# Dealing the last batch's shared expert out between the routed experts of a cross-attention and mixture-of-experts kernel

## The chip, the core and the metric

The kernel runs on one core of a Trainium2 chip. A core has five engines with an instruction stream each: TensorE (matmul, PE in the profile, its weight loads PEld), VectorE (DVE), ScalarE (ACT), GpSimd (POOL) and SyncE (SP), which here only issues transfers. Each engine works through its stream in order, and an instruction that waits holds up everything behind it on its engine. Transfers are issued from SP's queue or from GpSimd's and are carried out by 16 DMA engines that both queues share. The metric is the device time of one launch in microseconds (us), the median over runs; lower is better.

## The reference

All numbers are fp32. A batch of 4 sequences of 512 tokens of width 512 goes through a cross-attention layer and then through a mixture of experts; `out` is the sum of the residual and both.

```python
x = x + attention(layernorm(x), ctx)      # 16 heads of 32; 257 image keys and 1344 text keys, two softmaxes, summed
h = layernorm(x)                          # 2048 tokens
idx, w = router(h)                        # sigmoid scores, 3 of 8 groups, then 4 of 32 experts for each token
slots = the first 80 tokens of each expert, in order of token
for e in range(32):                       # routed experts, 512 -> 256 -> 512
    y = (silu(h[slots[e]] @ Wg[e]) * (h[slots[e]] @ Wu[e])) @ Wd[e]
    out[slots[e]] += y * w[slots[e]]
shared = (silu(h @ sg.T) * (h @ su.T)) @ sd.T     # shared expert, 512 -> 512 -> 512, every token
x = x + out + shared
```

## The kernel before

**Order of work.** The whole order is written out by hand: the program issues instructions in the order of its text, and each engine runs its own in that order. Semaphore waits are derived from which buffers and which regions of DRAM an instruction reads and writes. Two writes to overlapping regions of `out` are put in order by a wait, and a scatter to rows that are only known at run time counts as a write to all of `out`.

**Attention.** For each batch `b` there are four groups `c` of four heads each. A group walks over 13 tiles of keys (`t`, lines 632 to 680). For each tile `exps` (L370) makes scores and their exponentials `pT` in a *wide* buffer (128 x 4 x 512, 1 MB). Two tiles later `consume` multiplies them with the values, and one tile later `added` (L391) adds them up for the softmax's denominator; in the last group of a batch these additions run on VectorE. There are five wide buffers, used in turn (`wide`, L130); keys' weights, the output projection's weights `wo`, the shared expert's input `xT` and its hidden layer `hT` use the same five.

**Residual and routing.** `residual` (L446) projects a tile of 128 tokens, adds x, stores the sum `x1` in DRAM (`x1_d`, L461), normalizes it, and stores it in DRAM by rows (`xw_d`) and transposed (`xnT_d`). For the last batch this happens between the units of the shared expert. `routing` (L717) is a list of small VectorE instructions that end in lists of tokens for each expert; `first` is that of the first three batches, `second` that of the last one. The list's items are dealt out between the units: unit `i` may spend up to `(i - 1) * SHARE` in all, by costs that stand in L979. The ranks (L799) are transposes on TensorE that need a result of VectorE.

**Shared expert.** `shared` (L826) makes a list of units. For each batch there are four `gate` and four `up` units (each a projection of four matmul pairs into a PSUM bank, then Silu on ScalarE or a product on VectorE) and four `down` units (a projection, an addition of x1 fetched from DRAM, and a store to `out`). The downs of a batch stand between the gates and ups of the next. The first `xT` is loaded at L700, behind the last attention group. So there are 44 units before the tokens are known, and the four downs of the last batch (`last_downs`) run behind the issue of the first gathers.

**Routed experts.** For each expert `gather` (L877) fetches 80 rows by an indirect transfer on GpSimd's queue, four experts ahead. `turn` transposes them on TensorE two experts ahead, `gate_up` and `down` (L906) are the matmuls, and the 80 rows `y` are added to `out` in DRAM by an indirect transfer with an addition (L914), on GpSimd's queue. The weights of an expert (three transfers of 512 KB on SP's queue, L709) have four buffers of each kind and are loaded three experts ahead. In expert `e`'s turn the program issues `gate_up(e)`, `gather(e + 4)`, `turn(e + 2)`, `down(e - 1)`, and the weights of `e + 3`.

Of the kernel before, what the change touches and what calls it, by code (L numbers as in the profile page):

```python
# [9 lines left out]
F32 = mybir.dt.float32  # L10
# [3 lines left out]
ALU = mybir.AluOpType  # L14
# [4 lines left out]
P = 128  # L19
# [5 lines left out]
NC = D // P  # L25
# [78 lines left out]
def body(ctx, tc, a, ident, mhalf, logits, x1_d, xw_d, xnT_d, den_d, rec_d, out):  # L104
# [6 lines left out]

    w, mid = pool("w", 1), pool("mid", 1)
    kv, cx = pool("kv", 1, early, side="right"), pool("cx", 1, early, side="right")
    pt, hold, row, st = pool("pt", 5), pool("hold", 4), pool("row", 5), pool("st", 3)
    ring = pool("ring", 1, space=PSUM)
    banks = list(range(8))
    later = Later()
# [9 lines left out]
        n = banks.pop(0)  # L127
        return ring.tile([P, 512], F32, name="po", tag=f"bank{n}"), n

    def wide(name):  # L130
        return pt.tile([P, NC, 512], F32, name=name, tag="wide")

    def rowt(name):
        return row.tile([P, D], F32, name=name, tag="row")
# [311 lines left out]
    def residual(b, qt, aoT, wo):  # L446

        i = b * NQ + qt
        rows = slice(i * P, (i + 1) * P)
        t = {}  # L450

        def fetch():
            t["xr"] = load_x(b, qt)
            nc.gpsimd.tensor_tensor(t["xr"], t["xr"], o_b, ALU.add)

        def project_o():
            ps = psum()
            project(ps, lambda k: aoT[:, k, qt * P:(qt + 1) * P], lambda k: wo()[:, k, :])
            t["x1"] = rowt("x1")
            nc.vector.tensor_tensor(t["x1"], ps, t["xr"], ALU.add)  # L460
            nc.sync.dma_start(x1_d[rows, :], t["x1"])  # L461
            t["moments"] = moments(t["x1"])

        def norm():
            t["xn"] = rowt("xn")
            centred(t["xn"], t["x1"], t["moments"])
            nc.sync.dma_start(xw_d[rows, :D], t["xn"])

        def turn():
            ps = psum()  # L470
            for c in range(NC):
                nc.tensor.transpose(ps[:, c * P:(c + 1) * P], t["xn"][:, c * P:(c + 1) * P], ident)
            t["xnT"] = rowt("xnT").rearrange("p (c t) -> p c t", c=NC)
            nc.scalar.copy(t["xnT"], ps.rearrange("p (c t) -> p c t", c=NC))
            nc.sync.dma_start(xnT_d[:, :, rows], t["xnT"])

        def route():
            ps = psum()
            project(ps[:, :E], lambda k: t["xnT"][:, k, :], lambda k: rw[:, k, :])
            nc.vector.tensor_copy(logits[:, i, :], ps[:, :E])  # L480

        return fetch, project_o, norm, turn, route
# [23 lines left out]
    for b in range(B):  # L506
# [94 lines left out]
        for c in range(NC):  # L601
            more = c + 1 < NC
            if more:
                mx = st.tile([P, NQ, NG4, NM], F32, name="mx", tag="mx", bufs=2)
            if b == B - 1 and c == 0:
                sg = weight("shared_gate", tag="q_w")
            if b == B - 1 and not more:
                su, sd = weight("shared_up", tag="v_w"), weight("shared_down", tag="v_img_w")
            fill, done = [], 0
            pTs, outs, pos, g = [], [], [], {}  # L610

            def taken(pos=pos, outs=outs):
                po, n = pos.pop(0)
                o = held("po_s")
                nc.scalar.copy(o, po)
                banks.append(n)
                outs.append(o)

            def consume(t, v=v, pTs=pTs, pos=pos, taken=taken):

                if t in (0, MIX):
                    pos.append(kept())
                if t == MIX:
                    weighted(
                        v, t, pTs[t], (pos[0][0], slice(0, HALF), False, True), (pos[1][0], slice(HALF, P), True, False)
                    )
                else:
                    weighted(v, t, pTs[t], (pos[0][0], slice(0, key_rows(t)), t == 0, t == NKT - 1))
                if t in (MIX, NKT - 1):
                    taken()  # L630

            for t in range(NKT):
                pT = wide("pT")
                pTs.append(pT)
                if more:
                    wave(c + 1, t, qT, kT, mx)
                if t == 0 and c:
                    mT = shifts(part, nc.scalar.copy)
                if t in (0, 2) and pending:
                    pending.pop(0)()  # L640
                if t == 1:
                    if more:
                        v_next = kv.tile([P, NKT, P], F32, name="v", bufs=2)
                        fill = values(v_next, c + 1, cTs, ws)
                        fill[0]()
                        done = 1
                    elif b + 1 < B:
                        fill = work
                if t > 1:
                    consume(t - 2)  # L650
                exps(c, t, qT, kT, mT, pT)
                if t == 0 and pending:
                    pending.pop(0)()
                if t == 2:
                    g["acc"] = begun(pTs, not more)
                elif 2 < t <= MIX:
                    added(g["acc"], pTs[t - 1], slice(0, P), not more)
                elif t == NKT - 1 and not more:
                    added(g["acc"], pTs[MIX], slice(0, HALF), True)
                if c == 0 and t < 3:  # L660
                    rest[t]()
                if c == NC - 2 and b + 1 < B and t and t % 3 == 0:
                    turn[t // 3 - 1][2]()
                while t and done * (NKT - 1) < len(fill) * t:
                    fill[done]()
                    done += 1
                later.step()
                if more and t == NKT - 1:
                    part = parts[(c + 1) % 2]
                    split(mx, part, NM)  # L670
                if c == NC - 2 and b + 1 < B:
                    if t == 0:
                        xs = []
                        qT_next, sq_next, turn, work = queries(b + 1, xs, P)
                    if t % 3 == 0 and t < 3 * NQ:
                        xs.append(load_x(b + 1, t // 3))
                    if t % 3 == 1 and t < 3 * NQ:
                        turn[t // 3][0]()
                    if t % 3 == 2:
                        turn[t // 3][1]()  # L680

            def image(consume=consume, pTs=pTs, idle=not more):

                consume(NKT - 2)
                added(pTs[NKT - 2], pTs[NKT - 1], slice(0, key_rows(NKT - 1)), idle)
                if idle:
                    added(pTs[NKT - 2], pTs[MIX], slice(HALF, P), idle)

            def end(i=b * NC + c, c=c, aoT=aoT, outs=outs, acc=g["acc"], pTs=pTs, idle=not more):
                slabs = [(acc, 0), (pTs[NKT - 2], 2)] + ([] if idle else [(pTs[MIX], 1)])  # L690
                normalize(i, c, aoT, *outs, summed(slabs))

            pending += [image, partial(consume, NKT - 1), end]
            if more:
                v = v_next
            else:
                pending.pop(0)()
        if b + 1 < B:
            qT, sq_q = qT_next, sq_next
    first_xT = wide("xT")  # L700
    nc.sync.dma_start(first_xT, xnT_d[:, :, :L])
    aoT_last = aoT


# [6 lines left out]
        return ws  # L711

    NR = NT - NQ
    SHARE = 2.3
    AHEAD = 4

    def routing(lo, n):  # L717
# [108 lines left out]
    def shared():  # L826

        units = []
        downs = []
        xTs = {0: first_xT}  # L830

        def fetch_x(n):
            xTs[n] = wide("xT")
# [2 lines left out]
        for n in range(B):  # L836
# [11 lines left out]
            def up(ic, n=n, t=t):  # L848
                ps = psum()
                project(ps, lambda k: su[:, k, ic * P:(ic + 1) * P], lambda k: xTs[n][:, k, :])  # L850
                nc.vector.tensor_tensor(t["hT"][:, ic, :], t["hT"][:, ic, :], ps, ALU.mult)

            def fetch(j, n=n, t=t):
                t[j] = held("x1r")
                nc.sync.dma_start(t[j], x1_d[n * L + j * P:n * L + (j + 1) * P, :])

            def down(j, n=n, t=t, fetch=fetch):
                if j == 0:
                    fetch(0)
                if j + 1 < NQ:  # L860
# [3 lines left out]
                nc.vector.tensor_tensor(t[j], t[j], ps, ALU.add)  # L864
                nc.sync.dma_start(out[n * L + j * P:n * L + (j + 1) * P, :], t[j])

            for ic in range(NC):
                units += [partial(gate, ic), partial(up, ic)]
                if n and ic < 2:
                    units += downs[2 * ic:2 * ic + 2]  # L870
            downs = [partial(down, j) for j in range(NQ)]
        return units, downs

    def expert_parts():
        weights, xps, xpTs, hs = {}, {}, {}, {}
# [47 lines left out]

        return weights, gather, turn, gate_up, down

    units, last_downs = shared()
    wo = weight("o_w", wide("wo"))
    for u in units[:2]:
        u()
# [55 lines left out]
    tokens()  # L985
    for e in range(AHEAD):
        gather(e)
    for f in last_downs:
        f()
    turn(0)  # L990
    turn(1)
    for e in range(E + 1):
# [6 lines left out]
        if e:  # L999
            down(e - 1)  # L1000
            if e + 3 < E:
                weights[e + 3] = expert_weights(e + 3)

# [1 line left out]

# [34 lines left out]
```

## Time and profile before

| what | us |
|---|---|
| median of 3 runs | 1780.51 |
| lowest and highest run | 1779.47, 1783.83 |
| the profiled execution, end to end | 1803.62 |
| span of its records | 1801.9 |
| TensorE busy | 1709.7 (95%) |
| VectorE busy | 1002.6 (56%) |
| GpSimd busy | 830.4 (46%) |
| start of the first shared unit's matmuls | 1383.74 |
| start of the tokens' transpose | 1563.80 |
| start of the first expert's transpose | 1577.76 |
| last matmul's end | 1785.98 |

The profile shows one execution, and times in it count from the start of its span. A row of the timeline holds a start, a duration, the engine, the line of the code, what the instruction writes and reads, how many were merged, and in brackets how long the engine had been idle before it and what ended that. A row of waits holds who waited for whom, the total, how often, and the longest. Indirect transfers are issued from GpSimd; their rows show the time of issuing, not that of the transfer.

### The profile page before, as it was taken

What the parts mean: (1) busy time and instruction counts of PE and PEld (TensorE: products, weight loads), DVE (VectorE), ACT (ScalarE), POOL (GpSimd) and SP (SyncE); (2) the same over time, 40 slices, a digit from 0 to 9 for tenths busy, and PEclk for the clock granted to TensorE, in tenths of its full rate; (3) what the DMA queues carried; (4) which work ended last, traced back from release to release, by engine and by line L of the source; (5) the groups of instructions that cost most, each with busy time, mean ns of one, the idle gap of its engine ahead of it and who ended that gap; (6) DMA issues with size and microseconds to landing.
All of it is one profiled execution on the core that took longest, in us unless ns stands there. A gap on an engine that the chain in (4) does not pass through costs nothing. (4 is left out here: it accounts for less than half of the span.)

```text
span 1801.9 us, 29352 instructions
## 1 busy us (share of the span) xinstructions
PE 1709.7 (95%) x11825; PEld 899.0 (50%) x11825; DVE 1002.6 (56%) x1893; ACT 621.7 (35%) x1336; POOL 830.4 (46%) x564
## 2 busy tenths in 40 slices
PE   4999999999999999999999999998999999999886
PEld 2564444445644444565444445643442454477664
DVE  2485666658556657675566558556556668511110
ACT  1114444631254555114554631254456110011111
POOL 1319759322379662327679422377681100123332
PEclk9999999999999999999999999999999999999998
DMA  6000000040100003120001040300011363389894
GB/s 220 1 1 1 20 1 31 15 156 30 65 1 20 31 2 119 50 77 18 20 1 32 14 156 13 105 1 14 2 59 60 114 207 105 100 263 283 272 287 103
DMA packets 68023, 138.38 MB, mean 77 GB/s; under 512 B 16048, under 2 KB 28464, under 8 KB 65584
## 3 DMA queue, kind: packets, MB, share of 16 engines
q1 hardware_dynamic: 62768, 125.70, 20.7%
q0 software_dynamic: 5120, 10.82, 2.9%
q8 instruction: 93, 1.52, 0.3%
q14 instruction: 42, 0.34, 0.1%
HBM read 113.68 MB, written 22.81 MB: 76 GB/s over the span
## 5 line engine op out<-in xcount | busy, mean ns | idle before, releaser
L380 ACT ACTIVATE pT<-ps 128x512 f32<-128x512 f32 (+1 forms) x832 | 429.7, 603 | 385.7 <-PE ps L379 377.4
L342 DVE TENSOR_REDUCE mx<-ps 128x1 f32<-128x512 f32 (+1 forms) x576 | 330.5, 615 | 255.8 <-PE ps L328 255.8
L395 POOL TENSOR_TENSOR acc<-acc,pT 128x1024 f32<-128x1024 f32 x192 | 449.5, 2377 | 14.4 <-ACT pT L380 13.8
L298 PEld LDWEIGHTS ps<-v_w,cT 128*128 128x128 f32 (+1 forms) x1408 | 170.5, 188 | 103.2 <-DVE mx L342 55.3
L387 PE MATMUL po<-pT,v 128*32 128x512 f32 (+2 forms) x1792 | 221.9, 603 | 0.0
L379 PE MATMUL ps<-qT,kT 32*128 32x512 f32 (+1 forms) x1664 | 218.0, 594 | 0.0
L328 PE MATMUL ps<-kT,qT 32*128 32x512 f32 (+1 forms) x1536 | 205.1, 550 | 0.0
L298 PE MATMUL ps<-v_w,cT 128*128 128x128 f32 (+1 forms) x1408 | 199.0, 286 | 0.0
L238 PE MATMUL ps<-cT,wk 128*128 128x512 f32 (+1 forms) x384 | 153.9, 546 | 0.0
L316 DVE TENSOR_REDUCE mx<-ps 128x1 f32<-128x512 f32 (+2 forms) x256 | 128.2, 564 | 7.3 <-PE ps L313 7.2
L914 POOL DMA_INDIRECT out<-y,tok x32 | 45.4, 1420 | 146.4 <-DMA out<-y,tok 72.3
L376 PE MATMUL ps<-mT,pick 32*128 32x512 bf16 (+1 forms) x832 | 86.7, 386 | 23.0 <-DVE mx L342 19.6
L395 POOL TENSOR_TENSOR pT<-pT 65x1024 f32<-65x1024 f32 x24 | 56.0, 2352 | 109.1 <-PE po L387 89.4
L245 POOL TENSOR_TENSOR sq_k<-sq_k,sq 128x512 f32<-128x512 f32 (+2 forms) x48 | 49.6, 1033 | 122.6 <-ACT sq L242 122.6
L376 PEld LDWEIGHTS <-pick 32*128 32x128 bf16 (+1 forms) x832 | 21.8, 91 | 167.4 <-issue 164.1
L238 PEld LDWEIGHTS ps<-cT,wk 128*128 128x128 f32 x384 | 69.6, 190 | 70.5 <-issue 54.3
L904 DVE TENSOR_TENSOR ehT<-ehT,ps 128x160 f32<-128x160 f32 x32 | 10.3, 321 | 164.1 <-ACT ehT L903 164.1
L306 ACT COPY v<-ps 128x128 f32<-128x128 f32 (+1 forms) x208 | 59.7, 287 | 117.4 <-PE ps L298 116.8
L328 PEld LDWEIGHTS ps<-kT,qT 32*128 32x128 f32 x1536 | 80.4, 184 | 31.1 <-issue 10.4
L379 PEld LDWEIGHTS ps<-qT,kT 32*128 32x128 f32 (+1 forms) x1664 | 81.5, 181 | 27.4 <-issue 23.1
L387 PEld LDWEIGHTS po<-pT,v 128*32 128x32 f32 (+2 forms) x1792 | 34.6, 107 | 119.1 <-issue 109.8
L402 POOL TENSOR_TENSOR acc<-pT 128x1024 f32<-128x1024 f32 x24 | 56.7, 2386 | 79.8 <-ACT pT L380 55.3
(176 smaller groups left out, 2187.6 us busy)
## 6 DMA issues: line engine op xcount, KB each, us to landing
W_gate<-in_W_gate SPq DMA_DIRECT2D x32, 512.0 KB, 5.7
W_up<-in_W_up SPq DMA_DIRECT2D x32, 512.0 KB, 6.7
W_down<-in_W_down SPq DMA_DIRECT2D x32, 512.0 KB, 5.5
xt<-in_x SPq DMA_DIRECT2D x32, 256.0 KB, 2.8
cT<-in_ctxT SPq DMA_DIRECT2D x8, 1024.0 KB, 8.4
rb<-rec_d SPq DMA_DIRECT2D x64, 128.0 KB, 2.7
wk<-in_k_w SPq DMA_DIRECT2D x4, 1024.0 KB
wki<-in_k_img_w SPq DMA_DIRECT2D x4, 1024.0 KB, 10.2
```

Source lines behind the costliest of these rows:

```text
L238: nc.tensor.matmul(ps[:, :n], lhsT=wt[:, k, c * P:(c + 1) * P], rhs=xT[:, k, to], start=k == 0, stop=k == NC - 1)
L298: nc.tensor.matmul(ps[lo:hi, :], lhsT=cTs[bl][:, k, at:at + hi - lo], rhs=ws[bl == NB - 1][:, k, c * P:(c + 1) * P], start=k == 0, stop=k ...
L306: nc.scalar.copy(v[:n, t, :], ps[:n])
L316: nc.vector.tensor_reduce(mx[:, qt, g, bl:bl + 1], ps[:, :n], AX.X, ALU.max, negate=True)
L328: nc.tensor.matmul(ps[:, j * n:(j + 1) * n], lhsT=qT[r:r + HD, c, q * P:(q + 1) * P], rhs=kT[r:r + HD, c, k0:k0 + n], start=True, stop=True,)
L342: nc.vector.tensor_reduce(mx[:, qt, g, i:i + 1], ps[:, :m], AX.X, ALU.max, negate=True)
L376: nc.tensor.matmul(ps[:n], lhsT=pick[r:r + HD, kind(t), :n], rhs=mT[r:r + HD, :], start=True, stop=False)
L379: nc.tensor.matmul(ps[:n], lhsT=kT[r:r + HD, c, t * P:t * P + n], rhs=qT[r:r + HD, c, :], start=False, stop=True)
L380: nc.scalar.activation(pT[:n, g, :], ps[:n], AF.Exp)
L387: nc.tensor.matmul(po[r:r + HD, :], lhsT=v[rows, t, r:r + HD], rhs=pT[rows, g, :], start=start, stop=stop)
L395: (nc.vector if idle else nc.gpsimd).tensor_tensor(to[rows, h, :], to[rows, h, :], pT[rows, h, :], ALU.add)
L402: (nc.vector if idle else nc.gpsimd).tensor_tensor(acc[:, h, :], pTs[0][:, h, :], pTs[1][:, h, :], ALU.add)
```

## The change

The last batch's gate, up and down units are no longer part of the shared stage. They are returned as a list `between`, and one of its twelve items is issued at the end of each odd expert's turn, from expert 1 to expert 23. The last batch's `x1` is stored in `out` instead of `x1_d`; its down units copy their result to SBUF on ScalarE, and an accumulating transfer on GpSimd's queue adds it to `out` (128 rows of 2 KB), in place of the fetch of x1, the addition on VectorE and the plain store. The first `xT` is loaded in tile 6 of the last attention group, into one of the five wide buffers, which stays out of the turn until the last unit of the first batch that reads it. With 36 units in place of 44, `SHARE` is 2.9 in place of 2.3.

```diff
--- before.py
+++ after.py
@@ -111,7 +111,7 @@
 
     w, mid = pool("w", 1), pool("mid", 1)
     kv, cx = pool("kv", 1, early, side="right"), pool("cx", 1, early, side="right")
-    pt, hold, row, st = pool("pt", 5), pool("hold", 4), pool("row", 5), pool("st", 3)
+    pt, hold, row, st = pool("pt", 1), pool("hold", 4), pool("row", 5), pool("st", 3)
     ring = pool("ring", 1, space=PSUM)
     banks = list(range(8))
     later = Later()
@@ -127,8 +127,16 @@
         n = banks.pop(0)
         return ring.tile([P, 512], F32, name="po", tag=f"bank{n}"), n
 
-    def wide(name):
-        return pt.tile([P, NC, 512], F32, name=name, tag="wide")
+    wides = list(range(5))
+
+    def wide(name, keep=False):
+
+        n = wides.pop(0)
+        t = pt.tile([P, NC, 512], F32, name=name, tag=f"wide{n}")
+        if keep:
+            return t, n
+        wides.append(n)
+        return t
 
     def rowt(name):
         return row.tile([P, D], F32, name=name, tag="row")
@@ -458,7 +466,8 @@
             project(ps, lambda k: aoT[:, k, qt * P:(qt + 1) * P], lambda k: wo()[:, k, :])
             t["x1"] = rowt("x1")
             nc.vector.tensor_tensor(t["x1"], ps, t["xr"], ALU.add)
-            nc.sync.dma_start(x1_d[rows, :], t["x1"])
+
+            nc.sync.dma_start((out if b == B - 1 else x1_d)[rows, :], t["x1"])
             t["moments"] = moments(t["x1"])
 
         def norm():
@@ -664,6 +673,9 @@
                 while t and done * (NKT - 1) < len(fill) * t:
                     fill[done]()
                     done += 1
+                if b == B - 1 and not more and t == NKT // 2:
+                    first_xT = wide("xT", True)
+                    nc.sync.dma_start(first_xT[0], xnT_d[:, :, :L])
                 later.step()
                 if more and t == NKT - 1:
                     part = parts[(c + 1) % 2]
@@ -697,8 +709,6 @@
                 pending.pop(0)()
         if b + 1 < B:
             qT, sq_q = qT_next, sq_next
-    first_xT = wide("xT")
-    nc.sync.dma_start(first_xT, xnT_d[:, :, :L])
     aoT_last = aoT
 
 
@@ -711,7 +721,7 @@
         return ws
 
     NR = NT - NQ
-    SHARE = 2.3
+    SHARE = 2.9
     AHEAD = 4
 
     def routing(lo, n):
@@ -827,7 +837,7 @@
 
         units = []
         downs = []
-        xTs = {0: first_xT}
+        xTs = {0: first_xT[0]}
 
         def fetch_x(n):
             xTs[n] = wide("xT")
@@ -849,12 +859,21 @@
                 ps = psum()
                 project(ps, lambda k: su[:, k, ic * P:(ic + 1) * P], lambda k: xTs[n][:, k, :])
                 nc.vector.tensor_tensor(t["hT"][:, ic, :], t["hT"][:, ic, :], ps, ALU.mult)
+                if n == 0 and ic == NC - 1:
+                    wides.append(first_xT[1])
 
             def fetch(j, n=n, t=t):
                 t[j] = held("x1r")
                 nc.sync.dma_start(t[j], x1_d[n * L + j * P:n * L + (j + 1) * P, :])
 
             def down(j, n=n, t=t, fetch=fetch):
+                if n == B - 1:
+                    ps = psum()
+                    project(ps, lambda k: t["hT"][:, k, j * P:(j + 1) * P], lambda k: sd[:, k, :])
+                    y = held("ys")
+                    nc.scalar.copy(y, ps)
+                    nc.gpsimd.dma_start(out[n * L + j * P:n * L + (j + 1) * P, :], y, accum_op=ALU.add)
+                    return
                 if j == 0:
                     fetch(0)
                 if j + 1 < NQ:
@@ -864,12 +883,15 @@
                 nc.vector.tensor_tensor(t[j], t[j], ps, ALU.add)
                 nc.sync.dma_start(out[n * L + j * P:n * L + (j + 1) * P, :], t[j])
 
+            if n == B - 1:
+                return units + downs, [partial(f, ic) for ic in range(NC) for f in (gate, up)] + [
+                    partial(down, j) for j in range(NQ)
+                ]
             for ic in range(NC):
                 units += [partial(gate, ic), partial(up, ic)]
                 if n and ic < 2:
                     units += downs[2 * ic:2 * ic + 2]
             downs = [partial(down, j) for j in range(NQ)]
-        return units, downs
 
     def expert_parts():
         weights, xps, xpTs, hs = {}, {}, {}, {}
@@ -923,7 +945,7 @@
 
         return weights, gather, turn, gate_up, down
 
-    units, last_downs = shared()
+    units, between = shared()
     wo = weight("o_w", wide("wo"))
     for u in units[:2]:
         u()
@@ -985,8 +1007,6 @@
     tokens()
     for e in range(AHEAD):
         gather(e)
-    for f in last_downs:
-        f()
     turn(0)
     turn(1)
     for e in range(E + 1):
@@ -1000,6 +1020,8 @@
             down(e - 1)
             if e + 3 < E:
                 weights[e + 3] = expert_weights(e + 3)
+            if e % 2 and between:
+                between.pop(0)()
 
 # ---- launch: one core; the host lays the arrays out ----
```

## Prediction

> **What bounds the kernel now.** The share of busy time (TensorE 95%) is a mean over stages, so I first read the windows of each engine over the last 450 us, the part which the change touches, then the timeline of each of its joints, then who waited for whom. Columns of the windows: busy us and instructions of TensorE, weight loads, VectorE, ScalarE, GpSimd, then granted clock, DMA share, GB/s.
>
> ```profile
> 1400.00:1450.00 50.00, 50.00 (x130) 22.98 (x129) 35.55 (x63) 4.71 (x8) 10.18 (x12) 1.00 0.46 152
> 1450.00:1500.00 50.00, 50.00 (x151) 24.73 (x150) 35.21 (x45) 6.43 (x9) 1.80 (x3) 1.00 0.56 189
> 1500.00:1550.00 50.00, 49.46 (x119) 21.82 (x118) 43.09 (x95) 2.39 (x4) 0.00 (x0) 1.00 0.22 70
> ...
> 1630.00:1680.00 50.00, 44.64 (x290) 34.66 (x289) 5.32 (x14) 7.60 (x15) 16.55 (x15) 0.91 0.89 272
> 1680.00:1730.00 50.00, 45.23 (x306) 35.15 (x305) 5.23 (x14) 6.92 (x14) 16.39 (x14) 0.93 0.90 280
> 1730.00:1786.00 56.00, 50.15 (x326) 37.37 (x324) 6.15 (x16) 8.89 (x18) 19.26 (x16) 0.97 0.72 213
> ```
>
> In the shared-expert stage (to 1564) TensorE never rests and VectorE, which does the routing, is at 71 to 86%. In the expert stage (1578 on) TensorE loses time: clock below 1, DMA at 0.9. The waits of that stage say to whom:
>
> ```profile
> POOL out L914 <- DMA out<-y,tok: 72.3, 18, 6.0
> ...
> PE ps L890 <- DMA xp<-xw_d,tok: 17.7, 11, 2.6
> ```
>
> Each scatter-add (L914) waits on GpSimd for its predecessor to land, the gathers (L879) queue behind it, and TensorE's transpose (L890) waits 17.7 us for gathers. So this stage has two bounds close together. TensorE's own work is 5.53 us an expert:
>
> ```profile
> 1588.59 1.91 PE L232 MATMUL ps<-xpT,W_gate 128*128 128x80 f32 x16
> ...
> 1594.12 1.91 PE L232 MATMUL ps<-xpT,W_gate 128*128 128x80 f32 x16
> ```
>
> 1594.12 - 1588.59 = 5.53, times 32 = 177.0. The stage runs from 1577.8 to TensorE's end at 1786.0, 208.2, so 31.2 is **loss**: waits, and slow matmuls after them. The other bound is the chain of scatters, landing by landing: while weights stream, 4.8 to 8.7 us from start to start where the predecessor's landing was the releaser, mean 6.7; in the tail, without weights, 4.65:
>
> ```profile
> 1709.06 1.42 POOL L914 DMA_INDIRECT out<-y,tok  x1 [5.00 <-DMA out<-y,tok]
> 1710.79 0.93 POOL L879 DMA_INDIRECT xp<-xw_d,tok  x1 [0.30 <-issue]
> 1716.13 1.42 POOL L914 DMA_INDIRECT out<-y,tok  x1 [4.41 <-DMA out<-y,tok]
> ...
> 1789.73 1.39 POOL L914 DMA_INDIRECT out<-y,tok  x1 [3.25 <-DMA out<-y,tok]
> 1794.39 1.39 POOL L914 DMA_INDIRECT out<-y,tok  x1 [3.27 <-issue]
> ```
>
> **Profiled against plain.** That execution took 1803.6 (span 1801.9), 23.1 above the median of 1780.5. Matmuls back to back at 0.43 us can't hide that, so it sits where DMA landings set the pace: the start (0 to 25 us, DMA 0.93) and the expert stage. I put 17 of the 23 in the expert stage (26 scatters x 0.6 = 16, a chain of 6.1 in place of 6.7) and so take the loss in a plain run as 31.2 - 17 = 14. No row splits it; it is my largest unknown.
>
> **Step 1, the early load of the first xT.** Now TensorE meets this:
>
> ```profile
> 1383.74 6.49 PE L232 MATMUL ps<-xT,shared_gate 128*128 128x512 f32 x8 [3.81 <-DMA xT<-xnT_d]
> ...
> 1400.18 3.60 PE L232 MATMUL ps<-xT,shared_up 128*128 128x512 f32 x8
> ```
>
> The wait of 3.81 goes, and eight matmuls take 3.60 in place of 6.49: -6.7. The load takes one of five wide buffers for tiles 7 to 12, so an exp must wait for the additions four tiles back, not five. Tile 6's end at about 1372.7 (two of ten additions of 1.14 from 1370.37) and tile 10's exps start at about 1374.3 (ScalarE's row from 1370.01, 2.16 a tile): hidden with 1.6 to spare; without that cover one addition, 2.3. On SP the load stands behind rec and rb (1362 to 1364) and ahead of wo, which keeps its buffer and time; nothing queues behind it. Range -7 to 0.
>
> **Step 2, twelve units leave the shared stage.** Eight gate and up units before the tokens and four downs behind the gathers (1563.92, 14.00 us): 12 x 3.43 (1403.61 - 1400.18) = -41.2. Four x1 fetches and four stores leave SP, which isn't late there, and the last batch's x1 goes to `out` with the same store as before to x1_d: 0.
>
> **Step 3, routing in fewer units.** The share 2.9 in place of 2.3 deals the same list over units 2 to 31 rather than 39. By the code's own costs (63.9 for the first list, 23.0 for the second) the first ends at unit 23 and the second fills 23 to 31. The second list's VectorE rows add up to about 30 us (maxima and replacements 15, the 128-wide ones 9, small ones 4, gaps 2), evictions of those units add 5 x 0.65: 33.3 against 8 x 3.43 = 27.5 of TensorE. VectorE falls 6 behind; `ranks` (L802) and the first down, which needs the last product, make TensorE wait for it, with 1.5 of slow clock after it. Now it waits 0.54 there: +7. Ends: 0 if evictions catch up in the last four units, +11 if both waits are paid in full.
>
> **Step 4, the gathers lose their cover.** Now 14 us of downs lie between the gathers' issue (1564.5) and the first transpose (1577.8). Afterwards the transpose waits for the gather to land: 3.0 to 5.4 (least and median), I take 4.3. Whether slow matmuls follow, the Trainium skill and the rows see differently. The skill ("TensorE: Matmul & The Clock Gate", Part 1) has half clock only after an idle window of about 3.4 us, so a wait of 3.0 would cost 3.0 and no more. Here the down behind waits of 1.7 to 2.6 us took 2.7 to 3.6 in place of 1.88, six times of seven, 1.3 to 1.7 with the matmuls after it. By the row I add 1.7: +6; by the page's rule and the least landing it is +3. Ends +3 and +9.
>
> To the first transpose: -6.7 - 41.2 + 7 + 6 = **-34.9**.
>
> **Step 5, the units come back between the experts.** One after each odd expert to 23: +41.2 on TensorE. Its products and copies are 0.7 us on engines below 20%: 0. Whether 41.2 can sink into the old loss is the whole question. In the first half, a pair of experts takes 2 x 5.53 + 3.43 = 14.5 on TensorE against 13.4 on the chain: the loss vanishes there. In the second half (experts 16 to 31) four accumulating stores to `out` join the same chain at 17, 19, 21, 23: each waits on GpSimd for the scatter before it, the next gather and scatter wait behind it. The skill ("DMA: Bandwidth & Descriptors", Rules for kernel authors) gives the reason: an accumulate reads and writes later, so it must wait for the earlier DMA on those bytes; the 72.3 us above are that wait, and the row of a full-size store that adds is missing here. Its price: by the same page's fit (Anatomy of one DMA, 2.0 us + bytes / 436 per ns) 256 KB take 2.6. By the nearest row, scatters of 80 rows, least landing 3.8 and median 5.9, it is more for 128 rows. Uncontended, of 4.65 some 3 don't grow, 1.65 x 128 / 80 gives 5.6; contended, 3.6 x 1.6 = 5.8 and 3.0 give 8.8. I take 8.4; ends 3.4 (the page with 0.85 between landing and next issue) and 12.
>
> The second half in a plain run: chain 12 x 6.1 + 4 x 4.65 + 4 x 8.4 = 125; TensorE 16 x 5.53 + 4 x 3.43 = 102. GpSimd may end 7 later than without lag, as it does now (12.2 from TensorE's end to the last landing at 1794.39 + 3.8; 5.5 would do for one store), so the tail stays and 125 - 102 - 7 = 16 come back as loss; slow matmuls are inside it, since the chain sets the pace there. 16 against 14: +2. With the page's 3.4 the chain is 105, the loss 0 and this term -14.
>
> **Sum.** -34.9 + 41.2 + 2 = +8.3: 1780.5 + 8.3 = **1789**. In the profiled execution (chain 6.7, so 133 and a loss of 24 against 31) it would be about -1, so the two profiles may stand closer than the plain times.
>
> **Rivals.** (A) *The chain is the bound in plain runs too*, with a loss of 31, and the moved matmuls fill it. With stores of 6.5 rather than 8.4 the loss afterwards is 24 - 7.6 = 16: -34.9 + 41.2 + 16 - 31 = -9: 1771. For it: 72.3 us of waits, DMA at 0.9. Against: the 23 us. It decides from a plain period of 6.7 with stores below some 7.3. Faster, 0.20. (B) *It all cancels*: a plain period of 6.3 (loss 20) and stores of 7 leave 75.6 + 18.6 + 28 - 109 = 13: -1, 1780; 0.18. (C) *The stores bind harder*: 12 each with gathers behind them, 4 x 3.6 = 14 more: 1803; 0.14. For it: scatters of 8.7 already occur; against, they are few. (D) *The early load does nothing*, because buffer or transfer is late: 1789 + 6.7 = 1796; 0.06; against it stand the 1.6 us worked out above. The forecast has 0.42; with C and D, slower is 0.62. About 0.3% (5.3 us) is what a measurement of this kernel can tell from no change.
>
> The range runs from below A's middle to above C's, leaving out a third of A and half of C: 1768 to 1804. The forecast's own is 1786 to 1796.
>
> **What would show it.** Step 1: no wait on xT, first gate in 3.6. Step 2: twelve projections fewer before the first transpose. Step 3: TensorE waits at L802's transposes and the first down of the third batch, 4 to 11 us. Step 4: a wait for xp of 3 to 5 before the first transpose, which stands near 1543. Step 5: pairs of 14.5 without waits to expert 16, then waits for xp of 2 to 6 us around the accumulating stores; these 7 to 10 us apart from their neighbours; TensorE's end 235 to 250 after the first transpose (208 now). Wrong if the waits for xp in the second half are gone (A), or if VectorE isn't waited for.

## The result, and the profile after

| comparison with the kernel before, on the same chip | before, median (lowest to highest) | after, median (lowest to highest) | ratio, 95% interval |
|---|---|---|---|
| first, 12 runs each | 1782.41 (1779.05–1786.41) | 1807.05 (1788.14–1816.14) | 1.012 [1.0094, 1.0146] |
| second, another chip | 1787.32 (1781.63–1810.29) | 1804.85 (1786.73–1827.65) | 0.9991 [0.992, 1.0062] |

The ratios leave disturbed runs out, which in the second row takes away half of after's six, so its ratio is not that of the two medians beside it. In the first comparison the kernel became slower, by more than forecast: 24.6 us between the medians where the forecast had 8.3, and the median of 1807 stands 3 us above the top of the range (by the ratio, 1.012 x 1780.5 = 1802, it lies just inside). The two rows disagree by more than their intervals allow, and the lowest runs lie only 9 (first) and 5 (second) apart. So besides the change something else moves the time by 20 us and more. The profiles show both parts.

The profiled execution of after took 1808.05 (span 1806.3). First its TensorE timeline from the end of attention to the first experts:

```profile
1384.12 3.70 PE L240 MATMUL ps<-xT,shared_gate 128*128 128x512 f32 x8
...
1508.54 1.01 PE L812 MATMUL ps<-ident,chosen 128*32 128x128 f32 x4 [4.54 <-DVE chosen L790]
...
1544.00 0.80 PE L912 MATMUL ps<-ident,xp 80*128 80x80 f32 x4 [3.90 <-DMA xp<-xw_d,tok]
1545.11 0.77 PE L912 MATMUL ps<-ident,xp 80*128 80x80 f32 x4 [0.31 <-DMA xp<-xw_d,tok]
1545.67 3.62 PE L240 MATMUL ps<-xpT,W_gate 128*128 128x80 f32 x16
1549.08 3.62 PE L240 MATMUL ps<-xpT,W_up 128*128 128x80 f32 x16
...
1556.44 3.62 PE L240 MATMUL ps<-xpT,W_up 128*128 128x80 f32 x16
...
1560.39 3.22 PE L931 MATMUL ps<-W_down,ehT 128*80 128x512 f32 x4
1563.44 3.60 PE L240 MATMUL ps<-xT,shared_gate 128*128 128x512 f32 x8
1566.87 1.91 PE L240 MATMUL ps<-xpT,W_gate 128*128 128x80 f32 x16
...
1581.36 1.91 PE L240 MATMUL ps<-xpT,W_gate 128*128 128x80 f32 x16
```

The wait on `xT` is gone (step 1). TensorE waits 4.54 for VectorE at the ranks (step 3) and 3.90 for the first gather (step 4), and the first transpose starts at 1544.00. But then the gate and up groups of experts 0 and 1 take 3.62 each in place of the 1.91 that they take from 1566.87 on. Only behind the first matmuls that are 512 wide, expert 0's down at 1560.39, are they full speed again. From there a pair of experts with one shared unit takes 1581.36 - 1566.87 = 14.49, as forecast.

The windows of after confirm the clock (columns as in the prediction; the granted clock stands before the last two):

```profile
1545.60:1563.40 17.80, 17.80 (x79) 15.81 (x78) 1.94 (x5) 0.61 (x2) 1.82 (x2) 0.51 0.30 91
1563.40:1680.00 116.60, 116.60 (x707) 83.72 (x706) 14.39 (x36) 18.55 (x37) 37.70 (x32) 1.00 0.81 261
1680.00:1730.00 50.00, 47.65 (x268) 33.38 (x267) 4.42 (x12) 7.96 (x16) 13.01 (x11) 0.93 0.79 240
1730.00:1790.00 60.00, 51.62 (x321) 38.16 (x319) 5.25 (x14) 8.47 (x17) 19.93 (x17) 0.91 0.68 186
```

0.51 for 17.8 us, with TensorE busy all that time; then 116.6 us without any idle time; then losses from 1680 on, where the accumulating stores stand. Who waits there, from the list of waits of after, and TensorE's and GpSimd's rows around two of the four stores:

```profile
POOL out L936 <- DMA out<-y,tok: 36.4, 8, 5.4
POOL out L936 <- DMA out<-ys: 20.1, 4, 6.7
POOL out L875 <- DMA out<-y,tok: 18.2, 3, 6.5
```

```profile
1737.44 0.77 PE L912 MATMUL ps<-ident,xp 80*128 80x80 f32 x4 [2.18 <-DMA xp<-xw_d,tok]
...
1755.87 0.77 PE L912 MATMUL ps<-ident,xp 80*128 80x80 f32 x4 [5.64 <-DMA xp<-xw_d,tok]
...
1786.54 3.60 PE L931 MATMUL ps<-W_down,ehT 128*80 128x512 f32 x8
```

```profile
1742.40 1.44 POOL L936 DMA_INDIRECT out<-y,tok  x1 [1.96 <-ACT y L935]
...
1750.38 0.96 POOL L875 DMA_DIRECT2D out<-ys  x1 [6.54 <-DMA out<-y,tok]
1751.64 0.99 POOL L901 DMA_INDIRECT xp<-xw_d,tok  x1 [0.30 <-issue]
...
1756.14 1.47 POOL L936 DMA_INDIRECT out<-y,tok  x1 [3.52 <-DMA out<-ys]
```

The store at 1750.38 (L875) waits 6.54 for the scatter before it. Behind it stands the gather of expert 28, which is issued 6.5 late and lands at 1755.73, and TensorE's transpose for that expert, at 1755.87, has waited 5.64. TensorE ends at 1786.54 + 3.60 = 1790.1, 246.1 after the first transpose (208.2 before).

**Two parts of the time.** I split each profile at the end of the attention part (where the first shared gate could start). From there to the end of the span, before takes 422.0 and after 422.2; in two further profiles of the unchanged kernels, before takes 415.9 and after 424.5. So the part that the change edits is longer by some 4 us in the mean (419 and 423.4), by 0.2 in one pair and 8.6 in the other. The larger scatter comes from ahead of that point, from 1380 us of which only the buffers' turn in the last group was edited. In the four profiles the attention part ends at 1379.9 and 1382.7 (before) and at 1384.1 and 1401.4 (after). What it follows is one VectorE instruction, the sum at the end of a group (L438 before, L446 after). Timeline of before, GpSimd, VectorE, TensorE:

```profile
218.13 9.27 POOL L395 TENSOR_TENSOR acc<-acc,pT 128x1024 f32<-128x1024 f32 x4
218.51 9.44 DVE L438 SCALAR_TENSOR_TENSOR aoT<-po_s,v_b 128x512 f32<-128x512 f32 x1
228.60 0.58 PE L376 MATMUL ps<-mT,pick 32*128 32x512 bf16 x1 [6.48 <-DVE mx L342]
228.60 2.28 PE L379 MATMUL ps<-qT,kT 32*128 32x512 f32 x8
232.00 2.36 POOL L395 TENSOR_TENSOR acc<-acc,pT 128x1024 f32<-128x1024 f32 x1 [4.59 <-ACT pT L380]
```

And in the kernel of the first experiment below, which has the same code here:

```profile
219.64 16.68 POOL L403 TENSOR_TENSOR acc<-acc,pT 128x1024 f32<-128x1024 f32 x7
220.13 2.40 DVE L446 SCALAR_TENSOR_TENSOR aoT<-po_s,v_b 128x512 f32<-128x512 f32 x1
```

The same instruction on the same shapes takes 9.44 or 2.40. In the long case it ends 0.55 us behind GpSimd's fourth addition (218.13 + 9.27 = 227.40), when GpSimd has no further one to make: the next starts at 232.00. The maxima behind it on VectorE are late, and TensorE waits 6.48 and goes on slowly (eight matmuls in 2.28). The long case comes up at most once in each batch, at its first group:

| profile | long sums, of 4 | end of the attention part |
|---|---|---|
| early_only, cover_two, stores_aside, units_left_out | 0 | 1365.1, 1366.3, 1367.2, 1363.3 |
| before, before_again, after | 2 | 1379.9, 1382.7, 1384.1 |
| stores_together, together_covered | 3 | 1393.2, 1392.4 |
| after_again | 4 | 1401.4 |

(1401.4 - 1365.5) / 4 = 9.0 us each, and the count orders all ten profiles. The names are those of the experiments. That the long sums are the cause rests on this order and on a wait of 6.4 to 6.5 that TensorE has behind each of them, in every profile, and nowhere else; the last experiment takes the instruction away, but brings waits of its own.

### The profile page after: what moved, and what is told of

Its sections match the earlier page's. It is cut to its first block, busy times and chain, and to the rows that moved or that the text cites. A ratio compares the mean times of both kernels' runs of the same rounds, so it can differ in the third digit from the quotient of the medians.

```text
span 1806.3 us, 29363 instructions
## 1 busy us (share of the span) xinstructions
PE 1716.0 (95%) x11825; PEld 906.4 (50%) x11825; DVE 1001.5 (55%) x1889; ACT 623.7 (35%) x1340; POOL 835.4 (46%) x568
## 5 line engine op out<-in xcount | busy, mean ns | idle before, releaser
L387 PE MATMUL ps<-qT,kT 32*128 32x512 f32 (+1 forms) x1664 | 218.2, 594 | 0.0
L926 DVE TENSOR_TENSOR ehT<-ehT,ps 128x160 f32<-128x160 f32 x32 | 10.3, 321 | 187.2 <-ACT ehT L925 187.2
L384 PE MATMUL ps<-mT,pick 32*128 32x512 bf16 (+1 forms) x832 | 87.0, 386 | 24.0 <-DVE mx L350 19.4
L314 ACT COPY v<-ps 128x128 f32<-128x128 f32 (+1 forms) x208 | 60.0, 289 | 117.4 <-PE ps L306 116.6
```

Source lines behind the costliest of these rows:

```text
L314: nc.scalar.copy(v[:n, t, :], ps[:n])
L384: nc.tensor.matmul(ps[:n], lhsT=pick[r:r + HD, kind(t), :n], rhs=mT[r:r + HD, :], start=True, stop=False)
L387: nc.tensor.matmul(ps[:n], lhsT=kT[r:r + HD, c, t * P:t * P + n], rhs=qT[r:r + HD, c, :], start=False, stop=True)
```

## The experiments

Differences between profiles are taken over the stretch from the end of the attention part to the end of the span, where these stalls don't reach; "after" stands there for its mean of 423.4. Two profiles of one kernel differ there by 6.1 (before) and 2.3 (after), so a difference of a few us between single profiles is not certain.

**The early load alone.** Before, with only the early load of the first `xT` and the numbered buffers that it needs (as in the change, not repeated here); all units stay where they were.

```diff
...
+                if b == B - 1 and not more and t == NKT // 2:
+                    first_xT = wide("xT", True)
+                    nc.sync.dma_start(first_xT[0], xnT_d[:, :, :L])
...
-    first_xT = wide("xT")
-    nc.sync.dma_start(first_xT, xnT_d[:, :, :L])
...
```

> The kernel before with one part of the change: the first xT is loaded in tile 6 of the last attention group, everything else stays. My sum (step 1): the wait of 3.81 us and 2.9 us of half clock go, -6.7 us against before; the first gate starts right behind the last attention tile. If the buffer or the transfer is late (rival D) it is 0. If a slow clock at this place is a matter of luck and not of the wait, less than 5.

Measured: 1778.20 (1772.65 to 1782.01) against 1797.28 of before on that chip, ratio 0.988 [0.984, 0.992]. The stretch is 413.7, against 422.0 and 415.9 of before: -8.3 and -2.2, mean -5. The wait on `xT` is gone and the first gate takes 3.70, so -6.7 stands and rival D is out:

```profile
1365.09 3.70 PE L240 MATMUL ps<-xT,shared_gate 128*128 128x512 f32 x8
```

The other 14 of the 19 us can't be put down to the early load: this profile has no long sum, and before on that chip ran from 1786 to 1809, as it would if most runs had some. Those runs have no trace, so this is argued; after, with the same buffers and the same early load, has two and four. The profile also settles a second point. It took 1780.5, inside its own timed runs, and yet its expert stage lasts 1763.4 - 1556.3 = 207.1 from the first transpose to TensorE's end, a loss of 30.1 over the 177 of TensorE's own work.

**Cover for the gathers.** After, with the first two of the twelve units ahead of the first transpose, behind the issue of the gathers.

```diff
         gather(e)
+    for f in between[:2]:
+        f()
+    between[:2] = [lambda: None] * 2
     turn(0)
```

> The changed kernel, with the first two of the twelve moved units (one gate, one up, 6.9 us) issued between the gathers and the first expert's transpose instead of behind experts 1 and 3; the accumulating stores keep their places. Theory of the uncovered gathers: TensorE idles 3.9 us there, falls to half clock, and the experts' short matmuls leave it there until the first 512-wide unit 18 us later, which costs another 8.7. Then this kernel is 10 to 13 us faster than the changed one (about +12 against before), and all matmuls of experts 0 and 1 take 1.9 us a group. Rival, the chain of stores: the stores set the end, TensorE's gain is waited away behind experts 16 to 31, and the time stays within 4 us of the changed kernel's (+25 against before).

Measured: 1782.35 (1776.96 to 1786.01), ratio to before 0.9911 [0.9878, 0.9944]; stretch 409.5, 13.9 less than after's mean of 423.4. Its TensorE timeline:

```profile
1526.50 3.60 PE L240 MATMUL ps<-xT,shared_up 128*128 128x512 f32 x8
1529.93 0.72 PE L912 MATMUL ps<-ident,xp 80*128 80x80 f32 x8
1531.34 2.01 PE L240 MATMUL ps<-xpT,W_gate 128*128 128x80 f32 x16 [0.69 <-DVE xpT L914]
1533.19 1.95 PE L240 MATMUL ps<-xpT,W_up 128*128 128x80 f32 x16
1534.98 0.44 PE L912 MATMUL ps<-ident,xp 80*128 80x80 f32 x4
1535.26 1.95 PE L240 MATMUL ps<-xpT,W_gate 128*128 128x80 f32 x16
```

No wait, and the first experts at 1.95 to 2.01. The lost cover cost a wait of 3.90 and then half clock, with four groups at 3.62 - 1.93 = 1.7 more each and slow transposes and a slow down: from the first transpose to the end of expert 0's down after takes 1563.44 - 1544.00 = 19.4, where before takes 1588.59 - 1577.76 = 10.8, so 8.6 more. That makes 12.5 by the rows, against 13.9 by the stretch.

**Stores out of the chain.** After, with the last batch's shared expert written by a plain store to `x1_d`. The last batch's shared expert is missing from this output, as it is in the next experiment.

```diff
-                    nc.gpsimd.dma_start(out[n * L + j * P:n * L + (j + 1) * P, :], y, accum_op=ALU.add)
+                    nc.gpsimd.dma_start(x1_d[n * L + j * P:n * L + (j + 1) * P, :], y)
```

> The changed kernel, with the last batch's four down results written by plain stores on GpSimd's queue to the DRAM scratch of x1 instead of being accumulated in out, so that they join no chain of writes to out (the output lacks the last batch's shared expert). Forecast's step 5: the chain of the second half loses 4 x 8.4 us, the waits for gathers there (2.4, 2.2, 5.6 us and the half clock behind them, 6 us) go: 14 to 20 us faster than the changed kernel. Rival, the moved matmuls themselves cost the time because TensorE has no slack in plain runs: 0 to 6 us faster.

Measured: 1770.36 (1769.12 to 1773.66), ratio 0.984 [0.9803, 0.9878]; stretch 404.7, 18.7 less than after. Of the waits for `xp` behind the start one is left:

```profile
1742.33 0.47 PE L912 MATMUL ps<-ident,xp 80*128 80x80 f32 x4 [0.65 <-DMA xp<-xw_d,tok]
```

So the four stores as additions to `out` cost 18.7, 4.7 each, and they are what TensorE waits for in the second half. The edit takes two things away at once, the place in the chain and the addition: the same transfer lands in 3.9 when it is plain; in after the accumulating one takes 5.0 to 8.1, median 6.4, both above the 2.6 that the prediction's fit gave as an estimate. That the place in the chain has a part of its own is shown below, where the four additions stay and only their places change.

**Without the units.** After, with no unit between the experts.

```diff
     units, between = shared()
+    between = []
```

> The changed kernel with the twelve moved units left out altogether (the output lacks the last batch's shared expert). What it is faster by is the price of the units in their new place. If they cost only TensorE's own time: 41 us. If they sink into slack of the chain: 15 to 25 us. If the stores add waits on top: 50 to 55 us. Against the kernel before it would then stand at -16, +5 or -27 us.

Measured: 1754.25 (1750.31 to 1760.64), ratio 0.9754 [0.9713, 0.9794]; stretch 388.8, 34.6 less than after. The 41.2 of TensorE's time and the 18.7 of the stores cost 34.6 together, so about 25 of their 60 went into idle time that the chain of scatters leaves anyway: here its waits come to 82.0, in 21 scatters. The start shows half clock with no shared unit near, so it isn't the units that bring it:

```profile
1524.29 0.79 PE L912 MATMUL ps<-ident,xp 80*128 80x80 f32 x4 [3.88 <-DMA xp<-xw_d,tok]
...
1536.87 3.62 PE L240 MATMUL ps<-xpT,W_up 128*128 128x80 f32 x16
...
1540.82 3.62 PE L931 MATMUL ps<-W_down,ehT 128*80 128x512 f32 x4
```

**Both kernels again, and two repairs,** on another chip. The first two are unchanged.

> The changed kernel once more, on one chip with its experiments and with the kernel before. The kernel before took 1782 and 1797 us on two chips, so the price of the change is open until both are seen side by side a second time. Theory of fixed prices (uncovered gathers 12, stores 12 to 16, routing 6, against the early load's 7): again +15 to +25 against before, and 10 to 13 above the variant with two units as cover. Rival, two stalls of VectorE behind GpSimd in the attention part (9.4 us each in both first profiles, none in the experiments' profiles) come and go with the chip or the run: then the difference depends on which kernel draws them, and it may lie anywhere between 0 and +25.

> The kernel before itself, for a second profile and as a measure of what a kernel differs by from itself: 0 in time. Theory of the attention stalls: if its runs are near 1797 the profile shows one or two scalar_tensor_tensor of 9.4 us in the first 1380 us and TensorE waiting behind them; if near 1782, none of them. Rival: the difference between the chips sits in the expert stage, where the scatters land later: then the stretch from the first expert's transpose to the end is 224 us or more in a run of 1797.

Measured: after 1804.85, ratio 0.9991 [0.992, 1.0062], its profile the one with four long sums; before 1789.95 (1779.63 to 1804.08), ratio to itself 0.9998 [0.9938, 1.0059], two long sums. The 24.6 us of the first comparison aren't repeated: on this chip before itself ranges over 24 us. The profiles' stretches, 424.5 and 415.9, are the second pair used above.

The first repair keeps the four results and issues the four stores together, at expert 23, so that the chain is held up once:

```diff
-                    nc.gpsimd.dma_start(out[n * L + j * P:n * L + (j + 1) * P, :], y, accum_op=ALU.add)
+                    t[j] = y
+                    for i in range(NQ if j == NQ - 1 else 0):
+                        nc.gpsimd.dma_start(out[n * L + i * P:n * L + (i + 1) * P, :], t[i], accum_op=ALU.add)
```

> The changed kernel with the four accumulating stores issued together, behind expert 23, in place of one each behind 17, 19, 21 and 23. They go to different rows and so need not wait for each other; the chain of writes to out gets one landing of about 9 us more, not four. Theory of the chain: the waits for gathers in the second half (2.4, 2.2 and 5.6 us and the half clock behind them, 16 in all) shrink to one of 3 to 8: 6 to 12 us faster than the changed kernel. Rival, the four stores' bytes and GpSimd's time to issue them cost, not the landings: 0 to 3.

Measured: 1791.48 (1782.31 to 1810.56), ratio 0.9999 [0.9931, 1.0067]; stretch 415.6, 7.8 less than after. GpSimd's timeline:

```profile
1741.48 3.65 POOL L877 DMA_DIRECT2D out<-ys  x4 [3.74 <-DMA out<-y,tok]
1745.43 1.01 POOL L903 DMA_INDIRECT xp<-xw_d,tok  x1 [0.30 <-PE ps L914]
1757.85 1.47 POOL L938 DMA_INDIRECT out<-y,tok  x1 [11.41 <-DMA out<-ys]
```

Four stores now cost one wait of 3.74 and one of 11.41 in place of 38.3 (20.1 + 18.2). The second repair adds the cover:

> The changed kernel with both repairs: the first two moved units between the gathers and the first expert's transpose, and the four accumulating stores together behind expert 23. If both prices stand for themselves they add: 12 and 6 to 12 make it 18 to 24 us faster than the changed kernel, at or below the kernel with the early load alone. If one chain sets the end, the second repair gives under 4.

Measured: 1775.92 (1771.66 to 1798.83), ratio 0.9919 [0.986, 0.9978], stretch 404.7, 18.7 less than after and 14 less than before; 10.9 of it is the cover (415.6 - 404.7). By its median it beats both kernels on that chip, with three long sums in its profile.

**The long sum taken away.** To compare without the stalls, the sum leaves VectorE: GpSimd adds, ScalarE adds the bias. The same edit was made to before, to after, and to after with both repairs.

```diff
-                later.after(1, lambda: nc.vector.scalar_tensor_tensor(
-                    aoT[:, c, :], po_t, v_b[:, c:c + 1], po_i, ALU.add, ALU.add
+                nc.gpsimd.tensor_tensor(po_t, po_t, po_i, ALU.add)
+                later.after(1, lambda: nc.scalar.activation(
+                    aoT[:, c, :], po_t, AF.Identity, bias=v_b[:, c:c + 1]
```

> The kernel before, with the sum at the end of each attention group (text part + bias + image part, VectorE's scalar_tensor_tensor with two SBUF inputs) made by GpSimd's own addition behind its two products, and the bias added on ScalarE. Theory of the attention stalls: once a batch that instruction takes 9.3 us in place of 2.4, when it comes upon GpSimd's row of four additions, and costs some 9 us each time; off VectorE it can't. Then the runs stand within some 5 us of each other (those of before: 1780 to 1810), near 1780, and no profile has the stall. Rival, the spread comes from the expert stage's landings: it stays 20 us wide.

> The changed kernel with the same move of the sum. With the stalls gone from both, what is left between the two is the change: my sum said +8.3; the stretches from the first shared gate on, taken from the profiles, say +4 (423 against 419). Expected: +4 to +9 us against the kernel before with the sum moved, both with narrow spreads. If the change itself makes the stalls more likely or costs the 24.6 us of the first comparison: +20 or more.

> The changed kernel with both repairs (two units between the gathers and the first transpose, the four stores together behind expert 23) and the sum moved. From the profiles its stretch from the first shared gate on was 404.7 against 423 and 419: 18 faster than the changed kernel with the sum moved, 10 to 14 faster than the kernel before with the sum moved, so 1766 to 1770, with a narrow spread. If the added GpSimd work sets the pace in the attention part: 5 to 10 more for all three of these kernels.

| kernel with the moved sum | median (lowest to highest) | ratio to before | against the first row |
|---|---|---|---|
| before | 1804.62 (1801.13–1809.03) | 1.0118 [1.0099, 1.0136] | |
| after | 1813.49 (1811.18–1818.24) | 1.0173 [1.0154, 1.0191] | +8.9 |
| after, both repairs | 1794.37 (1791.44–1799.37) | 1.0066 [1.005, 1.0082] | -10.3 |

The three stand close together (spreads of 7 to 8 us), and none can have a long sum. That the jumps are gone is likely but not shown by these runs: before, on the same chip, had a single jump in twelve (1802.94, the others 1780 to 1787), so seventeen runs without one prove little.

The forecast of about 1780 for the first row missed because of the price of the edit itself. Compared with before at its best on that chip (1779.98), the moved sum costs over 20 us, more than even the rival that put GpSimd's pace in the way allowed. It is paid in the attention part, which ends at 1387.2, 1387.1 and 1390.7 in the three profiles, where kernels without a long sum have 1363 to 1367: TensorE there has three or four waits of 3.3 to 5.0 that early_only doesn't have. GpSimd is busier by 20 us (851.1 against 830.4), and its own additions now stand one sum later; why the waits come from that stays open. As a repair it is no gain.

Without the stalls after is 8.9 slower than before, and the repairs give 19.1 (1813.49 - 1794.37), as the 18.7 of the stretches said. But the +8.9 is not the whole change, because step 1 has nothing to save here. Before with the moved sum:

```profile
1373.12 0.58 PE L376 MATMUL ps<-mT,pick 32*128 32x512 bf16 x1 [5.02 <-ACT pT L380]
...
1387.22 3.70 PE L232 MATMUL ps<-xT,shared_gate 128*128 128x512 f32 x8
```

TensorE waits 5.02 for an exponential in the last tiles of attention (after with the moved sum: 4.95), and behind it the late load of `xT` isn't waited for: the first gate takes 3.70 without a wait. With the -6.7 that the early load saves in the unmoved kernel, +8.9 becomes about +2. The stretches of this pair say the same: 415.4 and 423.1, +7.7 without step 1.

## Why the prediction was wrong in size and right in direction

- **Step 1** (-6.7): as forecast in the rows; alone, -5 by the stretch.
- **Step 2** (-41.2): as forecast, twelve units fewer.
- **Step 3** (+7): 4.54 at the ranks, 0.17 at the first down and 1.26 of slow clock behind, about 6. Cause and place as forecast.
- **To the first transpose:** from the end of attention 197.83 before and 159.88 after, -38.0 (the repeated pair: 197.83 and 160.39). The forecast's -34.9 holds 1.7 of slow clock, which falls behind that point: -36.6. Right to within 1.4.
- **Step 4** (+6): the mis-sized term. The wait was 3.90, and 0.31 more behind it (forecast 4.3), but the clock stayed at 0.51 for 17.8 us: 8.6 in place of 1.7. Together that is 12.5, and 13.9 by the covered kernel, above the end of +9. I took the price of slow clock from downs, which are 512 wide and followed by more of the same. Behind this wait come four groups of 80-wide matmuls, and the first 512-wide one is 15 us away. The trace of before had no wait ahead of so many narrow groups.
- **"Profiled against plain"**, the step that failed. I put 17 of the 23 us between the profiled execution and the median into the expert stage and set the loss there at 14 in place of 31.2. The profile of the early load alone took 1780.5, an ordinary time of that kernel, with a loss of 30.1. The 23 us are mostly the two long sums in that profile, 2 x 9 = 18. The trace of before showed it: the sums at L438 in the first group of each batch take 9.4, 2.5, 2.5 and 9.4.
- **Step 5** (+41.2 and a loss of 16 against 14): pairs of 14.49 without waits up to expert 16, and then waits of 2.35, 2.18, 5.64 and 0.56 for `xp`, as told. Store to next scatter took 8.9, 6.9, 7.5 and 5.8, mean 7.3 where I had 8.4. But the loss was 31.2 before (27.4 in the repeated profile) and 246.1 - 218.2 = 27.9 after (31.8), half clock included: no clear gain or loss, and both some 12 to 17 above my figures, so the two errors cancelled. Without the 8.6 of half clock (9.0 in the repeated profile) the loss fell, from 31.2 to 19.3 and from 27.4 to 22.8, where I had it rise by 2: part of the moved work did sink into it, and the half clock of step 4 ate that gain.
- **Sum** (+8.3): +0.2 and +8.6 by the two pairs of stretches, about +2 by the moved sum with step 1 added, +9 and +5 between the lowest runs of the two comparisons. So the change costs between 0 and 9 us, about 5 in the mean of the five; no figure here tells it closer. The other 16 or more of the first comparison's 24.6 fit two long sums more in after than in before on that chip; the timed runs have no trace, so this is argued from the profiles, not shown. There all twelve runs of before lie within 7.4 us, and eleven of after's twelve at 1797 or above; on the chip of the first four experiments it was before that ran high. So which kernel draws the long sums changes with the chip, and whether the edit has a part in it stays open.

Rival A had the chain right: it set the pace in ordinary executions too, with a loss of 31. Its store price of 6.5 was low and it lacked the half clock. With A's own equation, stores of 7.3 and 6.9 more of slow clock in step 4, -9 + 4 x 0.8 + 6.9 = +1, near the +0.2 between the first pair of profiles, and below the +4 of the two pairs together. Rival C, 12 us a store, did not occur. The +8.3 had the direction right and was nearer to the truth than A's -9, but partly by luck: a loss that was put too low on both sides, a gain there that was missed, and a half clock that was put too small made up for each other.

## What to carry to other kernels

Before pricing a wait on TensorE, look at what runs behind it: narrow matmuls may stay slow for long, here for some 15 us until wide ones came, and two independent units that were only moved ahead of the wait saved some 11 to 14 us. Additions to memory that must follow each other are a chain; a further store in it held the next scatter up by its landing (5 to 8 us here) and everything queued behind it, and four such stores issued together, where they go to different rows, cost less than four apart. If a profile is slower than the runs, look in it for one instruction that has two durations before putting the difference on the profiler.

## What was not expected of the hardware

- **VectorE's sum behind GpSimd: 2.4 or 9.3 us.** The Trainium skill ("SBUF — State Buffer", SBUF: two separate sides) says that a VectorE instruction with two SBUF inputs and a GpSimd instruction exclude each other, and that whoever starts first holds the port pair for its whole instruction. That would let VectorE in after one addition, 9.27 / 4 = 2.3 us, and the short case agrees. In the long case it stays out for all four, until GpSimd pauses. The moment at which VectorE's instruction begins doesn't decide it: in the first groups of before it begins 0.37 to 0.39 us after GpSimd's first addition, in the long and in the short cases alike. What decides between the two, and why it changes with the chip and the run, stays open.
- **Half clock that work doesn't end.** The same skill ("TensorE: Matmul & The Clock Gate", Part 1) gives an idle window of about 3.4 us, and the wait of 3.90 lies above it. But for 15 us afterwards TensorE is busy in every record and still at 0.51, with 80-wide matmuls and a weight load for each; with the first 512-wide group it ended, in both kernels without cover that were shown. Before's first gate, eight 512-wide matmuls behind a wait of 3.81, was back at full speed by its end (6.49 in place of 3.60). That the width is what ends it is not shown: in both kernels it ends 19 to 20 us after the first transpose, and no run put wide matmuls right behind this wait.
